# A graph-attention layer on one core: one shared tile for the gathered rows of eight quads, in place of a pool of eight buffers

## The chip, the core and the metric

The kernel runs on one core of one Trainium2 chip. The time is that of the device for one execution, in microseconds (us). The kernel before took 2875.91 us, the median of three runs.

Names of engines: PE is TensorE (PEld its weight loads), DVE is VectorE, ACT is ScalarE, POOL is GpSimd, SP is SyncE, which issues most of the loads and stores.

## The reference

12500 nodes with 128 features, 200000 edges sorted by their destination, 64 features for each edge, four heads of 32. The layer computes, for each destination, a softmax over its edges and a weighted sum of the source rows:

```python
h = jnp.maximum(_layernorm(x), 0.0)
hn = (h @ W_node.T).reshape(num_nodes, H, HD)
e = (edge_features @ W_edge.T).reshape(num_edges, H, HD)
att = jnp.sum(jnp.concatenate([hn[src], hn[tgt], e], -1) * a, -1)
att = jnp.where(att > 0, att, 0.2 * att)
m = jnp.maximum(segment_max(att, tgt), 0.0)
ex = jnp.exp(att - m[tgt])
denom = segment_sum(ex, tgt) + (num_edges - deg)[:, None] * jnp.exp(-m)
out = x + segment_sum((ex / denom[tgt])[:, :, None] * hn[src], tgt)
```

## The kernel before

**Groups and quads.** The edges are cut into G = 392 groups of 511 edges and a place in front (GE = 512). A group's edges lie as J = 4 columns of 128 partitions. Four groups (QG) make a quad; there are nq = 98 quads. Destinations being sorted, a group's edges reach into a window of at most 96 nodes (WIN).

**Prologue.** The gathers of the first four quads (RAW) fetch rows of x itself, 64 of them. Meanwhile the node phase normalises all nodes, multiplies them by the weights and writes a table in HBM, with a row of ROW = 137 numbers for each node. From quad 4 on, gathers fetch rows of that table.

**Gathers.** `gather(q, rows, width)` issues one indirect DMA on POOL for each column of each group, 16 in a quad (L135). Each fetches 128 rows, as `srci` tells, into a tile `ga` of the pool `gath` (L129), which has eight buffers. The tile of quad q + 8 takes the place of quad q's. A tile that takes another's place waits until all that use the earlier one are done, so the first gather of quad q + 8 waits for the last use of quad q's tile; the other 15 follow in POOL's order. Nearly all that POOL does in the main loop is to issue these gathers.

**Logits.** `all_logits(q)` opens with `open_logits(q)`, which issues the loads of quad q + 2 on SP: `ea` and `db` (L281, L283), the four windows `pw` and `xw` (L466, L468), and its gathers on POOL. Each of its four steps then makes one group's marks `at` (L498, DVE) and its logits `lg` (L503, L506, PE). `add_sources(q)` adds the part that comes from the gathered rows (L518, L520, DVE). That is the first reader of a quad's gathers in the main loop.

**Softmax.** After each super, in the main part four quads, `softmax(s)` turns the logits, runs scans on DVE, and puts out the factors `ex_ps`, `xs` and `facs` that the sums use.

**Sums.** `sums(q)` takes the quad's groups in turn. For each one DVE multiplies the gathered rows by `ex` in place (L685) and writes the one-hot matrix `hot` (L689); PE multiplies the columns 1 to 3 into `acc` (L694). Column 0 carries over what the group before left unfinished, so `complete_group` follows one group later: DVE scales the carried row into `ga` (L633), ACT copies its count (L637), PE adds column 0 (L638), and ACT copies the sum out to `pt` (L639), from which the next group's carry is read. L638 is the last instruction that reads a group's part of `ga`. The chain L639, L633, L638, L639 goes from group to group. `divide` finishes a quad (L706 to L718), and SP stores four windows to `out` (L720).

**Order.** All engines run their instructions in the order in which the code issues them (`manual_schedule`); `together` deals out the steps of several generators in turn. In the main loop, a step of `sums` stands beside a step of `all_logits` of a quad four or five further on, and in the first quad of each super beside a step of the softmax too. Waits between engines are put in by the framework, from what each instruction reads and writes.

Of the kernel before, what the change touches and what calls it, by code (L numbers as in the profile page):

```python
# [8 lines left out]
F32 = mybir.dt.float32  # L9
# [6 lines left out]
P = 128  # L16
# [8 lines left out]
R_CNT, R_SRC, ROW = H * HW, H * HW + 1, H * HW + 5  # L25

J = 4
# [3 lines left out]
QG = 4  # L31
# [2 lines left out]
SIDE = PIECES * H  # L34
NODE_T = 9
RAW = 4
SETS = max(NODE_T, QG * J)
PAD = 1 << 20

# [6 lines left out]
def kernel(  # L46
# [41 lines left out]
    consts = ctx.enter_context(tc.tile_pool(name="consts", bufs=1))  # L88
# [30 lines left out]
    nq = len(quads)  # L119
    raw = RAW  # L120
    assert raw == 4 <= nq
    g_raw = sum(quads[raw - 1])
    gath = ctx.enter_context(tc.tile_pool(name="gath", bufs=8))
    GA = {}

    def gather(q, rows, width):

        g0, m = quads[q]
        ga = GA[q] = gath.tile([P, QG, J, ROW], F32, name="ga")  # L129
        for i in range(m):  # L130
            n = -(-min(E - (g0 + i) * NE + 1, GE) // P)
            if n < J:
                nc.vector.memset(ga[:, i, n:, :], 0.0)
            for j in range(n):
                nc.gpsimd.indirect_dma_start(  # L135
                    out=ga[:, i, j, 0:width], out_offset=None, in_=rows,
                    in_offset=bass.IndirectOffsetOnAxis(ap=srci[:, g0 + i, j:j + 1], axis=0))
# [8 lines left out]
    with tc.manual_schedule():  # L146

        nc.sync.dma_start(srci[:, :g_raw], src_by_edge[:, :g_raw])
        for q in range(raw):
            gather(q, x, D)  # L150
# [6 lines left out]
        with tc.tile_pool(name="prep", bufs=1) as prep, tc.tile_pool(  # L157
            name="prep_ps", bufs=1, space=bass.MemoryType.PSUM
# [21 lines left out]
        def statistics(pool, rows, T):  # L180


            assert nc.vector.BN_STATS_DIM == 6
            stats = pool.tile([P, SETS, 6], F32, name="stats")
            for t in range(T):
# [3 lines left out]
            two = stats[:, :T, :].rearrange("p t (o k) -> p t o k", k=3)  # L189
            both = pool.tile([P, SETS, 2], F32, name="both")  # L190
            nc.vector.tensor_tensor(both[:, :T, :], two[:, :, 0, 1:3], two[:, :, 1, 1:3], op=OP.add)
            apart = pool.tile([P, SETS], F32, name="apart")
            nc.vector.tensor_tensor(apart[:, :T], two[:, :, 0, 1], two[:, :, 1, 1], op=OP.subtract)
            nc.vector.scalar_tensor_tensor(apart[:, :T], apart[:, :T], D / 4, apart[:, :T],
                                           op0=OP.mult, op1=OP.mult)
            nc.vector.tensor_tensor(apart[:, :T], apart[:, :T], both[:, :T, 1], op=OP.add)
            rstd = pool.tile([P, SETS], F32, name="rstd")
            nc.scalar.activation(rstd[:, :T], apart[:, :T], AF.Sqrt, bias=eps, scale=1 / D)
            nc.vector.reciprocal(rstd[:, :T], rstd[:, :T])
            shift = pool.tile([P, SETS], F32, name="shift")  # L200
            nc.vector.scalar_tensor_tensor(shift[:, :T], both[:, :T, 0], -0.5, rstd[:, :T],
# [84 lines left out]
        with tc.tile_pool(name="node", bufs=2) as node, tc.tile_pool(  # L286
            name="node_ps", bufs=2, space=bass.MemoryType.PSUM
        ) as node_ps, tc.tile_pool(name="index", bufs=1) as index, tc.tile_pool(
            name="index_ps", bufs=1, space=bass.MemoryType.PSUM
# [146 lines left out]
    with tc.tile_pool(name="work", bufs=2) as work, \  # L436
# [33 lines left out]
        def fetch(q):  # L470
            if q not in EA:
                fetch_edges(q)
            fetch_windows(q)
            if q not in GA:
                gather(q, table, ROW)
# [537 lines left out]
```

## Time and profile before

| | |
|---|---|
| median of 3 runs | 2875.91 us (2864.28 to 2878.76) |
| the profiled execution's own time | 2883.22 us |
| its span, first to last instruction | 2881.3 us |
| busy: POOL, PE, DVE, ACT | 52%, 48%, 47%, 15% |
| granted clock of TensorE, mean | 0.539 |
| DMA, mean over the span | 104 GB/s |
| gathers from the table | 1502, mean 951 ns each on POOL |

In a row of the groups, the numbers after the bar are the busy time in us and the mean of one in ns; after the second bar stands the time that the engine was idle just ahead of such instructions, and what ended most of it. In a row of the waits, the three numbers are the total in us, the number of waits and the longest. In a timeline row, the first number is the start in us from the start of the span, the second the time in us; the idle time ahead of it and what ended that stand in brackets. A time on POOL for a gather is that of issuing it, not of the transfer.

### The profile page before, as it was taken

Reading aid. Unit: us, or ns where it says so; the run is one execution under the profiler, and the core shown is the slowest. Engines: PE = TensorE matmul, PEld = TensorE weight load, DVE = VectorE, ACT = ScalarE, POOL = GpSimd, SP = SyncE. Lnnn points to the kernel's source line nnn. Section 1 sums busy time; section 2 is a strip of 40 time slices with the busy share of each in tenths; the row PEclk is TensorE's granted clock in tenths of the full one; section 3 lists DMA queues with packets and bytes.
Section 4 is the critical chain, followed back from the end, with each engine's and each line's share of the span. In section 5 each row is a group of like instructions: output and inputs, shape, how many; then the busy total and the mean of one; then the engine's idle time right before and its main releaser. Section 6 shows DMA issues by size and latency. Waiting matters only on the chain.

```text
span 2881.3 us, 29151 instructions
## 1 busy us (share of the span) xinstructions
PE 1388.3 (48%) x7275; PEld 1250.2 (43%) x7275; DVE 1361.9 (47%) x3314; ACT 428.3 (15%) x1777; POOL 1509.0 (52%) x1608
## 2 busy tenths in 40 slices
PE   2524645445444454454454454444444544544466
PEld 1423544444444444344444444444444444443465
DVE  2524454444444454453454454454453544554477
ACT  1524111111111111111111111111110110111112
POOL 7152345555555455555555555556555556565612
PEclk9966555555555555555555555555555555555555
DMA  4333344444344343434444434434434434434330
GB/s 141 115 112 85 88 125 105 103 112 111 97 111 108 95 123 98 111 101 105 113 102 108 110 100 108 111 100 108 111 101 107 110 101 107 107 90 105 94 93 19
DMA packets 214493, 299.10 MB, mean 104 GB/s; under 512 B 86121, under 2 KB 162153, under 8 KB 204914
## 3 DMA queue, kind: packets, MB, share of 16 engines
q1 hardware_dynamic: 162512, 184.97, 23.6%
q0 software_dynamic: 50112, 109.65, 15.7%
q10 hardware_dynamic: 1698, 2.58, 0.3%
q8 instruction: 61, 1.00, 0.1%
q14 instruction: 110, 0.90, 0.1%
HBM read 270.49 MB, written 26.52 MB: 103 GB/s over the span
## 4 chain that ended last, share of the span: by engine, by line
another core or an unknown queue 25%; PE 13%; DVE 10%; issue 6%; ACT 2%; DMA 0%; ACTq 0%; DVEq 0%; SPq 0%; POOL 0%; POOLq 0%
PE acc L694 7%; PE lg L506 2%; PE acc L638 2%; DVE at L498 2%; DVE res L714 1%; DVE res L718 1%; ACT pt L639 1%; DVE ga L633 1%; DVE run L576 1%; DVE hot L689 1%; DVE ga L685 1%; PE lg L503 1%; DVE run L554 0%; PE acc L609 0%
## 5 line engine op out<-in xcount | busy, mean ns | idle before, releaser
L135 POOL DMA_INDIRECT ga<-table,srci x1502 | 1428.0, 951 | 1252.6 <-PE acc L638 711.2
L694 PE MATMUL acc<-ga,hot 128*97 128x137 f32 x2352 | 650.0, 448 | 737.6 <-ACT ga L678 592.5
L694 PEld LDWEIGHTS acc<-ga,hot 128*97 128x97 f32 x2352 | 519.3, 279 | 762.5 <-ACT ga L678 602.1
L633 DVE TENSOR_TENSOR ga<-pt,facs 1x132 f32<-1x132 f32 x384 | 111.2, 289 | 1010.9 <-ACT pt L639 799.0
L639 ACT COPY pt<-acc 97x137 f32<-97x137 f32 x392 | 107.1, 273 | 2058.5 <-remote 1328.2
L506 PE MATMUL lg<-wblk,ea 128*128 128x8 f32 x1568 | 405.9, 357 | 0.0
L506 PEld LDWEIGHTS lg<-wblk,ea 128*128 128x128 f32 x1568 | 378.4, 306 | 0.0
L638 PE MATMUL acc<-ga,hot 128*97 128x137 f32 x784 | 261.9, 437 | 168.4 <-issue 82.4
L503 PEld LDWEIGHTS <-at 96*128 96x128 bf16 x1568 | 214.4, 165 | 227.2 <-DVE at L498 136.0
L638 PEld LDWEIGHTS acc<-ga,hot 128*97 128x97 f32 x784 | 195.9, 282 | 182.8 <-issue 89.6
L685 DVE TENSOR_TENSOR ga<-ga,ex_ps 128x528 f32<-128x528 f32 x392 | 270.4, 690 | 8.6 <-PE ex_ps L599 8.2
L498 DVE TENSOR_TENSOR at<-const_ps,db 96x512 bf16<-96x512 f32 x392 | 267.1, 683 | 7.4 <-DMA db<-in_dst_dram 1.5
L503 PE MATMUL lg<-pw,at 96*128 96x12 bf16 x1568 | 169.3, 181 | 158.4 <-DVE at L498 113.6
L689 DVE TENSOR_TENSOR hot<-const_ps,slot 128x384 f32<-128x384 f32 x384 | 209.6, 546 | 0.0
L599 PE MATMUL ex_ps<-ident,ex 64*128 64x64 f32 (+2 forms) x112 | 18.6, 315 | 214.4 <-ACT ex L588 214.4
L599 PEld LDWEIGHTS ex_ps<-ident,ex 64*128 64x128 f32 (+2 forms) x112 | 13.8, 207 | 217.4 <-ACT ex L588 217.4
L373 PE MATMUL row_ps<-wcat,hT 128*128 128x137 f32 x198 | 41.9, 365 | 77.7 <-DVE hT L365 31.6
L637 ACT COPY ga<-pt 1x1 f32<-1x1 f32 x384 | 72.3, 188 | 10.4
L373 PEld LDWEIGHTS row_ps<-wcat,hT 128*128 128x128 f32 x198 | 35.5, 255 | 84.0 <-issue 44.6
L135 POOL DMA_INDIRECT ga<-in_x_dram,srci x64 | 60.6, 947 | 20.8 <-issue 19.2
L714 DVE TENSOR_TENSOR res<-pt,const_ps 96x512 f32<-96x512 f32 (+1 forms) x101 | 67.4, 667 | 7.3 <-DMA out_dram<-res 3.5
L718 DVE TENSOR_TENSOR res<-res,xw 96x512 f32<-96x512 f32 (+1 forms) x99 | 66.7, 674 | 3.4
(133 smaller groups left out, 1036.2 us busy)
## 6 DMA issues: line engine op xcount, KB each, us to landing
db<-in_dst_dram SPq DMA_DIRECT2D x98, 768.0 KB
ea<-in_edge_t_dram SPq DMA_DIRECT2D x98, 512.0 KB
ga<-table,srci POOLq DMA_INDIRECT x1502
xw<-in_x_dram SPq DMA_DIRECT2D x392, 48.0 KB
out_dram<-res SPq DMA_DIRECT2D x392, 48.0 KB
pw<-side SPq DMA_DIRECT2D x392, 2.2 KB
table<-row SPq DMA_DIRECT2D x9, 616.5 KB
xt<-in_x_dram SPq DMA_DIRECT2D x9, 576.0 KB
```

Of the source, the lines that this page charges most:

```text
L135: nc.gpsimd.indirect_dma_start(out=ga[:, i, j, 0:width], out_offset=None, in_=rows, in_offset=bass.IndirectOffsetOnAxis(ap=srci[:, g0 + i, ...
L498: nc.vector.tensor_tensor(at[:, i, :], node_ps[0:WIN, g0 + i:g0 + i + 1].to_broadcast([WIN, GE]), db[:, i, :], op=OP.is_equal)
L503: nc.tensor.matmul(lg[:, i, j].rearrange("p k h -> p (k h)"), at[:, i, j * P:(j + 1) * P], sw, start=i + j == 0, stop=False, skip_group_ch ...
L506: nc.tensor.matmul(lg[:, i, 2 * w:2 * w + 2, 0, :], ea[:, i, w, :], wblk, start=False, stop=True, skip_group_check=True)
L633: nc.vector.tensor_tensor(ga[0:1, i, 0, 0:H * HW].rearrange("p (h w) -> p h w", w=HW), before[WIN:WIN + 1, 0:H * HW].rearrange("p (h w) -> ...
L638: nc.tensor.matmul(acc, hot[:, i, 0, :], ga[:, i, 0, :], start=False, stop=True)
L639: nc.scalar.copy(pt[:, i, :], acc)
L685: nc.vector.tensor_tensor(val, val, heads(ex)[:, :, :, g - s0].unsqueeze(3).to_broadcast([P, J, H, HW]), op=OP.mult)
L689: nc.vector.tensor_tensor(hot[:, i, :, 0:WIN], lane_ps.unsqueeze(1).to_broadcast([P, J, WIN]), slot[:, g, :].unsqueeze(2).to_broadcast([P, ...
L694: nc.tensor.matmul(acc, hot[:, i, j, :], ga[:, i, j, :], start=j == 1, stop=False)
L714: nc.vector.tensor_tensor(res[:, :n, :].rearrange("p g (h d) -> p g h d", d=HD), val[:, :, :, 0:HD], share_ps[:, :n, :].unsqueeze(3).to_br ...
L718: add.tensor_tensor(res[:, :n, :], res[:, :n, :], xw, op=OP.add)
```

## The change

The pool `gath` with its eight buffers goes. In its place one tile `ga_all` holds eight parts of a quad's size, and quad q takes the part q modulo 8. The dimensions of a part, and the bytes in all, are those of the eight buffers. Since all quads' rows now lie in one tile, the framework tells from the parts that instructions read and write who has to wait: a group's first gather waits for the uses of that group's place, not for those of the quad.

```diff
+QUADS = 8
...
-    gath = ctx.enter_context(tc.tile_pool(name="gath", bufs=8))
+
+    ga_all = consts.tile([P, QUADS, QG, J, ROW], F32, name="ga")
     GA = {}
 
     def gather(q, rows, width):
 
         g0, m = quads[q]
-        ga = GA[q] = gath.tile([P, QG, J, ROW], F32, name="ga")
+        ga = GA[q] = ga_all[:, q % QUADS]
         for i in range(m):
```

## The prediction

> **What bounds the kernel now.** I read the page first, then the waits, then the timelines of GpSimd and ScalarE over one quad, then the rows of line L520. The page:
>
> ```profile
> span 2881.3 us, 29151 instructions
> PE 1388.3 (48%) x7275; PEld 1250.2 (43%) x7275; DVE 1361.9 (47%) x3314; ACT 428.3 (15%) x1777; POOL 1509.0 (52%) x1608
> ...
> L135 POOL DMA_INDIRECT ga<-table,srci x1502 | 1428.0, 951 | 1252.6 <-PE acc L638 711.2
> ...
> L639 ACT COPY pt<-acc 97x137 f32<-97x137 f32 x392 | 107.1, 273 | 2058.5 <-remote 1328.2
> ```
>
> No engine is busy for much over half of the span, so waits set the time. ScalarE stands idle for 2058.5 us ahead of the copy L639, and most of that ends with "remote", which no instruction of this core explains. The waits by total:
>
> ```profile
> ACT pt L639 <- remote: 1328.2, 113, 18.6
> DVE ga L633 <- ACT pt L639: 800.6, 155, 14.4
> POOL ga L135 <- PE acc L638: 711.2, 80, 56.6
> ```
>
> VectorE waits behind L639 (L633 reads its output), and TensorE behind both. POOL's own long wait is the one that the change edits. One quad shows how these hang together; POOL first, then ACT:
>
> ```profile
> 1771.81 0.94 POOL L135 DMA_INDIRECT ga<-table,srci  x1 [5.80 <-PE acc L638]
> 1773.06 0.94 POOL L135 DMA_INDIRECT ga<-table,srci  x1 [0.30 <-issue]
> ...
> 1790.68 0.94 POOL L135 DMA_INDIRECT ga<-table,srci  x1 [0.30 <-issue]
> 1797.53 0.94 POOL L135 DMA_INDIRECT ga<-table,srci  x1 [5.90 <-PE acc L638]
> ```
>
> ```profile
> 1771.57 0.27 ACT L639 COPY pt<-acc 97x137 f32<-97x137 f32 x1 [1.67 <-PE acc L638]
> ...
> 1774.49 0.28 ACT L639 COPY pt<-acc 97x137 f32<-97x137 f32 x1 [2.18 <-PE acc L694]
> ...
> 1778.50 0.27 ACT L639 COPY pt<-acc 97x137 f32<-97x137 f32 x1 [3.51 <-PE acc L694]
> ...
> 1794.44 0.27 ACT L639 COPY pt<-acc 97x137 f32<-97x137 f32 x1 [15.45 <-remote]
> ...
> 1797.29 0.27 ACT L639 COPY pt<-acc 97x137 f32<-97x137 f32 x1 [1.67 <-PE acc L638]
> ```
>
> A quad's 16 gathers start together, 1.25 us apart, right after the last group of the quad eight before is summed. Three groups get through beside them, 2.9 to 4.0 us apart. The next matmul L638 ended at 1781.38, but L639, which waits for nothing except that matmul, started at 1794.44: 13.06 us later, 2.5 us after the burst of gathers was over (1790.68 + 1.25). For each of the 392 groups I took the time from the end of L638 to the start of L639. Its median is 0.04 us and the sum 1151 us, 40% of the span. It depends on the age of the unbroken burst when L638 ends: at 2 to 3 us the median is 0.04 (57 groups), at 6 to 7 it is 0.42 (56), at 8 to 9 it is 6.3 (27), at 9 to 10 it is 13.04 (51), at 12 it is 10.6 (4), at 18 it is 4.4 (6). From 9 us on, age plus delay is nearly always 22 to 23 us, that is the burst's 20.0 us and 2.6 more. So in a burst older than about 7 us TensorE's signal mostly stays out until POOL pauses. I call that the freeze; its cause I do not know.
>
> This makes a locked cycle: 20.0 us of gathers, 2.6 until the frozen signal arrives, 3.1 until the quad's last group is summed (1794.44 to 1797.53), which starts the next burst: 25.7 us for each plain quad, as 1771.81 to 1797.53 shows. Where a softmax lies in the quad (one in four) it is 32.4. Gathered data itself is late for nobody that matters. Of L520, the first reader of a gather:
>
> ```profile
> L520 DVE TENSOR_TENSOR U<-st,ga x98: 266/268/302, 260.0 to 2833.1; 128x64 f32<-128x64 f32 x98
> its engine sat idle before it (us, times) until:
>   ACT ga L261: 20.9, 1
>   DVE st L518: 0.6, 3
> ```
>
> **The change, part by part.** *Instructions.* Order and count on PE, DVE, ACT and SP stay as they are, and so do their waits; no transfer is added, moved or resized. SP's queue of loads and stores is untouched, and POOL's order too. The 1.1 MB of gathers a quad stay the same. The allocation is the same size and costs nothing at run time.
>
> *POOL's waits.* Before, the first gather of each of the 90 quads 8 to 97 waits for the L638 of the fourth group of the quad eight before. After, the first gather of each group (360) waits for the L638 of the same group there; the fourth group's wait is the old one. So the first three groups may start about 9, 6 and 3 us earlier within the fast part, or earlier still by the length of a freeze. Behind a waiting gather only later gathers are queued on POOL (and the last two quads' L662 and L718), and none is let go later than before. The built program has 271 more waiting instructions on POOL. The row of L135 gives 17 ns as the median of one (POOLq EVENT_SEMAPHORE x93: 17/17/43); 271 x 17 ns = 4.6 us, and they lie in POOL's idle time or in its 0.30 us gaps. Bounds 0 and 5 us; I take 0, since POOL idles for 5.8 us a quad. If that idle time is gone they cost the 5.
>
> *What early gathers do by themselves.* Nothing: L520 lost 0.6 us to them in 98. The Trainium skill says, in DMA: Bandwidth & Descriptors, section Issuing engines are not separate DMA queues, that issuing takes time that is usually small beside the transfer. The trace differs here: a quad's issue takes 20.0 us of POOL, while the page gives q0, the gathers' queue, 15.7% of 16 engines, 4.6 us of each quad (2881.3 x 0.157 / 98). By the rule only the landing counts, and the change is worth 0: 2883 us. By the row the issue itself sets the cycle, and its new shape has to be worked out.
>
> *What the new shape of the bursts does.* Start where a frozen signal arrives (time 0). It releases L639 and now also four gathers, 5.0 us. The next groups follow as the ACT timeline has them, 2.9, 2.9 and 4.0 us apart (mean 3.2): at about 3 and 6 us, each letting go four more gathers. At age 6 a signal is delayed by 0 to 0.5 us, so these two pass. The third comes at 9 to 10 us and freezes. POOL has twelve gathers: it stops at 15.0, and the frozen signal arrives at 17.6. Three groups in 17.6 us are 5.87 each, 23.5 for a quad instead of 25.7: 2.2 saved. The gain is the 3.1 us in which POOL waited for the fourth group after the signal was back, spread over a cycle of three groups. What is late next is the same signal again: the freeze stays, with shorter bursts. A third signal that slips through early (age 8 to 9, delay 6.3) joins the next four gathers to the burst: 22.6 us for four groups, 5.65 each, nearly the same.
>
> Does a freeze come sooner after a shorter pause? The new pause is 2.6 us. Ten bursts before follow pauses of 2.7 to 3.0 us instead of 5.6, and signals at ages of 4.1 and 6.1 still passed in 0.0 to 0.1 us. So I take no.
>
> The softmax quads: POOL is let go by groups further apart than its 5 us, so it pauses between. If they keep their whole extra time, they save 2.2; with no freeze left but the one ahead, their own steps as the timeline has them (3.4 + 5.5 + 9.2 after the delivery, and about 9 for the third group with a rest of freeze) make 27, a saving of 5.4. No row decides; I take the middle, 3.8.
>
> *The sum.* Four quads save 3 x 2.2 + 3.8 = 10.4 us; 90 quads make 22.5 fours: 234 us. The two open bursts of 64 gathers at the start (3.1 and 161.6) and the last eight quads have no such wait and keep their time. The profiled execution took 2883.2 us (its span of 2881.3 and 1.9 around it), 7 over the median of the runs, 2875.9. So 2649 against 2883, or 2642 us as the median.
>
> The Trainium skill also has a price for TensorE's signals: TensorE: Matmul & The Clock Gate, section The cost: per-tile semaphore tail, says that increments queue at about 26.3 ns each. A group's ten counts would then delay L639 by about 0.26 us, 392 groups by 0.10 ms, no burst would matter, and breaking it up would gain nothing (2883). The row says 0.04 us outside a burst and 13 in an old one; I go by the row.
>
> **The rivals.**
> 1. *Every group freezes (slower).* If after a short pause the freeze sets in before the next group is through (2.85 us), each group has four gathers and a wait: 5.0 + 2.6 = 7.6 us, against 6.43 now (25.7 / 4). That is 30.4 a quad, 90 x 4.7 = 423 us more: 3300. It turns to a loss once about one group in three goes so, (6.43 - 5.87) / (7.6 - 5.87). For it: POOL is issuing in a greater share of the time, and no burst before follows a whole run of short pauses. Against: the ten bursts above.
> 2. *The freeze takes the second group too.* Two groups in 12.6 us: 25.2 a quad, 0.5 saved, softmax quads 2: 3.5 a four, 79 us, 2797. For it: a few signals at 6.7 us were late by 1.9.
> 3. *No freeze is left.* If it needs many ready gathers in a row and not elapsed time, POOL's rate bounds: 20.0 a plain quad, 24.1 a softmax quad; 3 x 5.7 + 8.3 = 25.4 a four, 572 us: 2304. Against: groups come every 3.2 us while four gathers take 5.0, so POOL would soon run unbroken.
> 4. *The early gathers are hidden anyway.* The freeze follows something else that only coincides with the bursts, such as SP's issues of pw and xw: no change, 2876. Against: age plus delay is constant to 1 us.
>
> **How the numbers follow.** My case has 0.55, rival 2 0.13, rival 3 0.10, rival 4 0.05, rival 1, whole or in part, 0.17. Faster by over 0.5%, about what a measurement of this kernel can tell from no change: 0.78; within it 0.05; slower 0.17. The likeliest case alone, with softmax savings of 2.2 to 5.4 and late signals, spans 2560 to 2720. The range takes in rivals 2 and 4, the slow end of rival 3 and the mild end of rival 1: 2430 to 2900.
>
> **What would show it.** Right: GpSimd's timeline in runs of about 12 gathers, with waits ahead of the first gather of a group; plain quads 23 to 24 us apart; the "remote" wait of L639 still there, most waits 7 to 9 us and no longer 13 to 15; DVE, PE and SP busy times as they were. Wrong: freezes of L639 at burst ages under 4 us (rival 1), POOL unbroken and L639's waits gone (rival 3), or delays as long as before although POOL paused (rival 4).

## The result, and the profile after

The changed kernel takes 2566.27 us (median of four runs, 2556.94 to 2567.05) against 2870.1 us (2863.71 to 2878.76) for the kernel before, measured together: a ratio of 0.8932, 95% interval 0.8896 to 0.8968. The forecast was 2642 us, with a range of 2430 to 2900. On another chip, told further below, the same two kernels take 2051.0 and 2046.7 us, and the change is worth 0.2%; on two more the kernel before takes about 2050 us too. The gain belongs to the chip as much as to the kernel.

The page of the kernel after (every line of the code stands two lower than before: L641 is the old L639, L640 the old L638, L137 the old L135):

```profile
span 2564.4 us, 29422 instructions
PE 1396.5 (54%) x7275; PEld 1246.7 (49%) x7275; DVE 1360.6 (53%) x3314; ACT 427.9 (17%) x1777; POOL 1514.3 (59%) x1608
...
L137 POOL DMA_INDIRECT ga<-table,srci x1502 | 1433.4, 954 | 925.2 <-issue 404.5
...
L641 ACT COPY pt<-acc 97x137 f32<-97x137 f32 x392 | 107.1, 273 | 1662.7 <-remote 904.7
```

The busy times are those of before, within 9 us on each engine; only idle time went. POOL's idle time ahead of gathers fell from 1252.6 to 925.2 us, ScalarE's ahead of the copy from 2058.5 to 1662.7. The waits, by total, the number of them and the longest:

```profile
ACT pt L641 <- remote: 904.7, 103, 11.8
DVE ga L635 <- ACT pt L641: 468.5, 141, 11.1
...
POOL ga L137 <- remote: 226.6, 102, 3.3
```

"Remote" is still the first wait, but its longest is 11.8 us and not 18.6. The last row has grown: POOL itself now waits for a late signal 102 times and not 10, 226.6 us and not 32.3, but never for more than 3.3 us. Its old wait for L638, 711.2 us and up to 56.6 at a time, is down to 136.5 us and 13.8. GpSimd's timeline over one burst, then ScalarE's over the same time:

```profile
1629.80 0.94 POOL L137 DMA_INDIRECT ga<-table,srci  x1 [1.33 <-PE acc L640]
...
1643.68 0.94 POOL L137 DMA_INDIRECT ga<-table,srci  x1 [0.30 <-issue]
1647.17 0.94 POOL L137 DMA_INDIRECT ga<-table,srci  x1 [2.54 <-remote]
```

```profile
1629.57 0.27 ACT L641 COPY pt<-acc 97x137 f32<-97x137 f32 x1 [1.58 <-PE acc L640]
...
1632.48 0.27 ACT L641 COPY pt<-acc 97x137 f32<-97x137 f32 x1 [2.18 <-PE acc L696]
...
1636.49 0.27 ACT L641 COPY pt<-acc 97x137 f32<-97x137 f32 x1 [3.51 <-PE acc L696]
...
1646.93 0.27 ACT L641 COPY pt<-acc 97x137 f32<-97x137 f32 x1 [9.95 <-remote]
```

The burst that starts at 1629.80 has twelve gathers and ends at 1644.6. Three groups come through at 1629.57, 1632.48 and 1636.49; the fourth stays out until 1646.93, 2.3 us after the burst. The next burst starts 17.37 us after the first one. That is the cycle of the prediction, 17.6 us for three groups.

From here on "late time" is the time from the end of L638 to the start of L639, or of their counterparts, summed over the 392 groups; 14 us is its floor, 0.04 for each. (The end of a matmul is modelled in the profile. The same model gives the floor in every trace without gathers or from another chip.) A "burst" is a run of gathers with less than 0.9 us between them. "A four" is the mean time of four quads, from quad 21 to quad 84. All three are worked out from the starts and ends in the traces. A "signal" is the count that a finished matmul raises and that others wait for.

| kernel | late time | bursts, most frequent | a four |
|---|---|---|---|
| before | 1152 us | 89 of 16 | 108.7 us |
| after | 816 us | 69 of 12, 58 of 8, 20 of 4 | 94.7 us |

14.0 us saved in each of 22.5 fours is 315 us; the two profiled executions differ by 317 (2883.2 and 2566.2).

### The profile page after: what moved, and what is told of

Its sections match the earlier page's. It is cut to its first block, busy times and chain, and to the rows that moved or that the text cites. A ratio compares the mean times of both kernels' runs of the same rounds, so it can differ in the third digit from the quotient of the medians.

```text
span 2564.4 us, 29422 instructions
## 1 busy us (share of the span) xinstructions
PE 1396.5 (54%) x7275; PEld 1246.7 (49%) x7275; DVE 1360.6 (53%) x3314; ACT 427.9 (17%) x1777; POOL 1514.3 (59%) x1608
## 4 chain that ended last, share of the span: by engine, by line
another core or an unknown queue 31%; PE 19%; issue 17%; DVE 15%; ACT 5%; POOL 4%; SPq 2%; DMA 1%; DVEq 0%; ACTq 0%; POOLq 0%
PE acc L696 10%; POOL ga L137 4%; PE lg L508 4%; PE acc L640 3%; DVE at L500 2%; ACT pt L641 2%; DVE res L716 1%; DVE res L720 1%; DVE hot L691 1%; DVE ga L687 1%; DVE run L556 1%; DVE ga L635 1%; PE lg L505 1%; ACT ga L639 1%
## 5 line engine op out<-in xcount | busy, mean ns | idle before, releaser
L137 POOL DMA_INDIRECT ga<-table,srci x1502 | 1433.4, 954 | 925.2 <-issue 404.5
L696 PEld LDWEIGHTS acc<-ga,hot 128*97 128x97 f32 x2352 | 515.7, 278 | 372.1 <-ACT ga L680 168.5
L640 PE MATMUL acc<-ga,hot 128*97 128x137 f32 x784 | 265.6, 442 | 263.1 <-ACT ga L639 127.8
L641 ACT COPY pt<-acc 97x137 f32<-97x137 f32 x392 | 107.1, 273 | 1662.7 <-remote 904.7
L640 PEld LDWEIGHTS acc<-ga,hot 128*97 128x97 f32 x784 | 190.7, 279 | 291.8 <-ACT ga L639 142.1
L520 DVE TENSOR_REDUCE st<-lg 128x64 f32<-128x192 f32 x98 | 33.7, 344 | 124.7 <-remote 79.9
L601 PE MATMUL ex_ps<-ident,ex 64*128 64x64 f32 (+2 forms) x112 | 18.6, 315 | 110.5 <-ACT ex L590 65.4
L639 ACT COPY ga<-pt 1x1 f32<-1x1 f32 x384 | 72.4, 188 | 10.7
L137 POOL DMA_INDIRECT ga<-in_x_dram,srci x64 | 60.6, 947 | 20.8 <-issue 19.2
L601 PEld LDWEIGHTS ex_ps<-ident,ex 64*128 64x128 f32 (+2 forms) x112 | 13.8, 208 | 113.5 <-ACT ex L590 67.4
```

The lines of the kernel that those rows point to most:

```text
L137: nc.gpsimd.indirect_dma_start(out=ga[:, i, j, 0:width], out_offset=None, in_=rows, in_offset=bass.IndirectOffsetOnAxis(ap=srci[:, g0 + i, ...
L639: nc.scalar.copy(ga[0:1, i, 0, R_CNT:R_CNT + 1], before[WIN:WIN + 1, R_CNT:R_CNT + 1])
L640: nc.tensor.matmul(acc, hot[:, i, 0, :], ga[:, i, 0, :], start=False, stop=True)
L641: nc.scalar.copy(pt[:, i, :], acc)
L696: nc.tensor.matmul(acc, hot[:, i, j, :], ga[:, i, j, :], start=j == 1, stop=False)
```

## The experiments

The twelve kernels ran in four sets, each beside the kernel before on the same chip. The results number the chips. The first set ran on chip 7, where the kernel before took 2874.8 us. The runs of the result carry no number; their 2870.1 us for the kernel before are like chip 7's, and they are counted with it here. The others fell to chips 15, 8 and 6, where it took 2049.3, 2051.0 and 2051.4.

### Chip 7: is it the shape of the bursts?

**The same tile, with the old waits** (e1_last_first). The last group's gathers are put first, so that all 16 wait for the whole quad again.

```diff
-        for i in range(m):
+        for i in ((m - 1, *range(m - 1)) if q >= QUADS else range(m)):
```

> The changed kernel, but POOL issues a quad's gathers with the fourth group first. Its wait is the quad's last one, so all sixteen follow it together, as before the change; tile, count and bytes stay those of the changed kernel. If the shape of the bursts makes the gain (my theory): back to 2840 to 2890 us, bursts of 16, L641's long waits 13 us again. If the shared tile itself, or anything but the waits, makes it: 2550 to 2590 us.

Measured: 2866.53 us, 0.9978 of before (0.9956 to 1.0). Its row of the gathers and its first waits:

```profile
L137 POOL DMA_INDIRECT ga<-table,srci x1502 | 1432.0, 953 | 1232.1 <-PE acc L640 684.3
```

```profile
ACT pt L641 <- remote: 1248.7, 114, 18.0
POOL ga L137 <- PE acc L640: 684.3, 78, 60.7
```

89 bursts of 16 and a late time of 1120 us are back, and so are POOL's 684.3 us of waits for L640, the longest 60.7, and ScalarE's longest of 18.0. The tile is still shared, the instructions of PE, DVE, ACT and POOL are as many as in the changed kernel and differ only in order, and the gain is gone. It comes from the finer waits, not from the tile.

**Half of the change** (e1b_pairs). Groups are gathered in the order 1, 0, 3, 2, so that two go at a time.

```diff
-        for i in range(m):
+        for i in ((1, 0, 3, 2) if q >= QUADS and m == 4 else range(m)):
```

> The changed kernel, with the groups' gathers issued in the order second, first, fourth, third, so that eight are let go at a time. My cycle: the second group's signal comes back by 6 us, joins another eight to the burst, the third group freezes until about 22 us, and the fourth has to be summed before POOL may go on: about 25 us for four groups, 2780 to 2870 us, nearly all of the gain gone. If instead the time follows the mean wait that POOL is spared, half of the gain: about 2720 us.

Measured: 2708.12 us, 0.9424 (0.9381 to 0.9468); 69 bursts of 16, 41 of 8, late time 983 us, a four of 101.4. Half of the change brings half of the gain: the number of the second expectation, and more than my cycle allows. Quad by quad, each taken from one fourth L640's end to the next (medians), that expectation's reason does not fit. The two plain quads ahead of a softmax quad take 25.8 us each, unchanged, as the cycle says for pairs. The softmax quad and the next one take 22.5 and 26.9 where the same kernel with the old waits (e1_last_first) has 32.4 and 22.2, and the kernel before 32.4 and 25.7. Most of what this kernel gains, it gains where a softmax stretches the steps.

**No gathers** (e3_plain_loads). From quad 4 on, the 16 gathers of a quad are four plain loads of table rows on SP. The output is then not the layer's: the choice of rows is left out.

```diff
             for j in range(n):
+                if q >= RAW:
+                    if j == 0:
+                        t0 = (4 * (g0 + i)) % 96
+                        nc.sync.dma_start(ga[:, i, 0:n, :], by_tile(table, t0, n))
+                    continue
```

> The kernel before, but from quad 4 on the rows of a group come by one plain load on SP from consecutive rows of the table, in place of four gathers on POOL. The same bytes go over the same DMA engines, with four more issues on SP for each quad; the rows are the wrong ones, which leaves out the gathering. If POOL's run of gathers makes the freeze (my theory): the waits of L639 that end in remote fall from 1328 us to under 100, quads come 13 to 20 us apart, 1700 to 2100 us in all. If SP's issues or the DMA traffic make it: the delays stay, 2600 us and up.

Measured: 2014.73 us, 0.7016 (0.699 to 0.7042). Its waits:

```profile
...
ACT pt L644 <- PE acc L643: 1295.4, 392, 13.5
PEld L508 <- DVE at L503: 426.0, 98, 9.6
...
DVE res L719 <- DMA out_dram<-res: 313.1, 63, 8.3
```

No wait of L644 ends with "remote" any more; all 392 end with the matmul L643. The late time is 14 us, its floor. The next waits are TensorE's for VectorE's marks (L503) and VectorE's for the stores of `out` (L719). On this chip the late signals need the gathers.

**A short pause for each group** (e4_pause). One memset on POOL after each group's four gathers.

```diff
+    rest = consts.tile([P, 128], F32, name="rest")
...
+            if q >= QUADS:
+                for _ in range(1):
+                    nc.gpsimd.memset(rest, 0.0)
```

> The changed kernel, with one small memset on POOL after each group's four gathers[...], which breaks the run of gathers every 5 us. If a short break is enough to hold off the freeze: L641's remote waits under 200 us, a group each 5.5 us, 2400 to 2450 us. If the freeze goes by the share of time that POOL issues, or needs about 2 us of rest to clear: bursts lengthen by the memsets, 6.0 to 6.2 us a group, 2590 to 2650 us.

Measured: 2581.85 us, 0.8982 (0.8947 to 0.9017), late time 912 us, 87 bursts of 12. The memset takes 0.22 us and moved the gather behind it by only 0.08, because it lies in the gap of 0.30 us that follows every gather. It was no pause, the time lies between the two forecasts, and it decides nothing. A longer one was tried next, but the chip was another.

### Chip 15: no late signals at all

**Column 0 last** (e7_cols). A group's columns 1 to 3, free a little earlier than column 0, are gathered first.

```diff
-            for j in range(n):
+            for j in (*range(1, n), 0):
```

> The changed kernel with the columns of a group gathered in the order 1, 2, 3, 0. Columns 1 to 3 are read last by L696, which runs a group step before L640, so three of the four gathers are let go about 1 us sooner. My cycle counts gathers in a burst and the time after it, and neither changes: 2540 to 2590 us. If a finer release goes on paying: 2500 us or less.

Measured: 2045.7 us, 0.9978 (0.9967 to 0.9989) of a kernel before that takes 2049.3 us here. The late time is 14 us, and the 1502 gathers of the main part form one burst. The edit's own question can't be answered where no signal is late.

**Fewer bytes** (e8_narrow). Each gather from quad 8 on moves 16 numbers a row and not 137; the other columns keep earlier rows.

```diff
             for j in range(n):
+                at = slice(0, width)
+                if q >= 2 * RAW:
+                    at, rows = slice(ROW - 16, ROW), x.rearrange("n (k c) -> (n k) c", c=16)
                 nc.gpsimd.indirect_dma_start(
-                    out=ga[:, i, j, 0:width], out_offset=None, in_=rows,
+                    out=ga[:, i, j, at], out_offset=None, in_=rows,
```

> The changed kernel, but from quad 8 on each gather fetches 16 numbers of a row (64 bytes) and not 137 (548 bytes), taken from x; the other columns keep what was there. POOL issues as many gathers of as many rows. If the issue of the gathers makes the freeze: delays and cycles as in the changed kernel, 2500 to 2590 us. If the bytes that they move make it: the delays shrink with the bytes, 2300 us or less.

Measured: 2041.88 us, 0.9955 (0.9939 to 0.9972). POOL is busy for 1519.8 us, against 1521.4 in e7_cols with all the bytes: a gather's 1.25 us does not depend on its bytes.

**A long pause** (e5_pause10). Ten memsets in place of e4_pause's one.

> The changed kernel with ten memsets on POOL after each group's four gathers. The first of them lies in the gap of 0.30 us that follows a gather anyway (one memset in e4 took 0.22 us and moved the next gather by 0.08), so the rest is about 2 us. If the freeze needs an unbroken run of gathers and a rest of about 2 us clears it (my theory): L641 waits for L640 nearly never over 1 us, but a group takes at least 7.1 us, 90 x 4 x 7.1 = 2560 us for the gathered part, 2950 to 3050 us in all. If the freeze goes by the share of time that POOL issues (70% here): the delays stay near those of the changed kernel, 816 us in all.

Measured: 3036.25 us, 1.4805 (1.4775 to 1.4835). The bursts are four long, as meant, but there was no late signal for a pause to cure, and the pauses cost 2.8 us each (3.07 between two bursts in place of 0.30) on a POOL that has no idle time here.

**Seven parts** (e6_seven). `QUADS = 7`.

> The changed kernel with seven parts in the tile, not eight: a group's gathers wait for the group seven quads back, so they come a quad later as seen from their first reader. If only the shape of the bursts counts: 2555 to 2580 us. If the head start of the gathers over their readers had a part in the gain: over 2600 us, with waits on DMA ahead of L522.

Measured: 2644.8 us, 1.2911 (1.288 to 1.2941). With seven parts, the gathers of a quad stand in the code ahead of the sums that still need its place, so these sums take the rows of a quad seven later and wait for them. It is not the kernel with less room that I meant, and its time says nothing. Its trace does say something: it has 76 bursts of 16 with pauses of 6.1 us (median) between them, the shape of the kernel before on chip 7. In these bursts 121 matmuls L640 ended at an age of 12 us or more, and none of their signals was over 0.04 us late. So it is not the shape of the bursts that sets chip 15 apart.

### Chips 8 and 6: is chip 15 the odd one?

**The changed kernel again** (f1_after), unaltered, with f2_narrow (e8_narrow again) and f3_pause10 (e5_pause10 again).

> The changed kernel, unaltered, beside the kernel before on whatever chip is given. If the chip is like the first one (the kernel before near 2870 us): 2566 us, ratio 0.893, late signals of TensorE summing to about 816 us, bursts of 12, 8 and 4. If it is like the second one (the kernel before near 2049 us): no late signal (each under 0.1 us), POOL gathering without a pause, 20 us a quad, and 2044 to 2049 us, ratio 0.997 to 1.0; the gain of the change is then gone although every instruction is the same. If the gain came from the coarser release by itself and not from the late signals, the ratio is near 0.9 on any chip.

Measured: 2046.73 us, 0.9984 (0.9974 to 0.9994) of 2051.02. Of its page and its waits:

```profile
span 2044.7 us, 29422 instructions
PE 1366.3 (67%) x7275; PEld 1237.5 (61%) x7275; DVE 1363.9 (67%) x3314; ACT 428.0 (21%) x1777; POOL 1523.3 (75%) x1608
...
POOL 7577777777777777777777777777777777777774
...
L137 POOL DMA_INDIRECT ga<-table,srci x1502 | 1441.0, 959 | 469.4 <-issue 389.1
...
L641 ACT COPY pt<-acc 97x137 f32<-97x137 f32 x392 | 107.4, 274 | 1268.0 <-PE acc L640 1268.0
```

```profile
ACT pt L641 <- PE acc L640: 1268.0, 392, 14.0
...
DVE U L522 <- DMA ga<-table,srci: 424.8, 77, 12.2
```

The instructions are those of the 2566 us kernel, 29422 of them. The same row L641 has no "remote" at all. POOL's digits are 7 from end to end: 1441.0 us of gathers and 469.4 of gaps are 1910 of the 2044.7 us, 1.27 us for each of the 1502 gathers, which all lie in one burst. No signal is more than 0.04 us late in it. The data itself is now what VectorE waits for: 424.8 us ahead of L522, where the kernel before had no wait for a gather ahead of its counterpart L520 on the first chip. POOL has become the bound.

> The changed kernel with each gather of quad 8 and later moving 16 numbers a row in place of 137 (the other columns keep the rows of earlier quads), so a gather moves 8 KB and not 70 KB. On a chip with late signals: if the lateness comes from POOL's making of the gathers (1.25 us each, which e8_narrow showed does not depend on the bytes), bursts and delays stay and it takes 2540 to 2590 us; if it comes from the bytes on the way (the DMA rings or the memory filled), the delays go and it takes about 2045 us, the POOL bound. On a chip without late signals: 2042 us again, which tells nothing apart.

Measured: 2043.97 us, 0.9974 (0.9963 to 0.9986). As announced for a chip without late signals, it tells nothing more.

> The changed kernel with ten more memsets on POOL after every group's four gathers, which cost 2.6 us a group where no signal is late (3036 us). On a chip with late signals: if a signal comes out as soon as POOL is out of gathers for a moment (over 0.3 us), every burst is 4 gathers long, no signal is late by more than about 1 us, and the time is again 3036 us within 1%, though the same signals are late by 816 us in all without the pauses; if the gathers' number or bytes outstanding is what counts, and not their unbroken run, signals stay late by several us each and the time is 3150 us or more.

Measured: 3037.74 us, 1.4825 (1.48 to 1.485). It equals 3036 us within 1%, but with no late signal to remove this is no support for either reading.

**The old waits and fewer bytes together** (f4_last_narrow): the edits of e1_last_first and e8_narrow.

> The changed kernel with the last group's gathers first (so that a whole quad's gathers wait for the whole quad, as in the kernel before) and with 16 of 137 numbers a row moved from quad 8 on (the other columns keep the rows of earlier quads). On a chip with late signals (the kernel before near 2870 us): if POOL's unbroken run of gathers makes the signals late, 89 bursts of 16 and late signals of about 1120 us in all stay, and it takes 2850 to 2870 us; if the bytes on the way do, the delays go and it takes about 2045 us. On a chip without late signals (the kernel before near 2050 us): 2040 to 2055 us; and since 16 gathers take 20.0 us there and a plain quad's sums come free before POOL has issued the 16 gathers ahead of them, POOL should show pauses of under 2 us a quad even where it waits for whole quads, which would say why the change is worth at most 0.5% there.

Measured: 2047.82 us, 0.9973 (0.9957 to 0.9989), on chip 6. The bytes stay undecided, since nothing is late here either. The other half was answered:

```profile
POOL ga L140 <- issue: 449.3, 1474, 0.3
```

Even where 16 gathers wait for a whole quad, POOL stands still only for the gap of 0.3 us between two gathers: 1390 of them form one burst. Releasing places group by group offers POOL something that it doesn't need. That is why the change is worth 0.2% on a chip where no signal is late.

## Why the prediction was right, and what it did not know

*The locked cycle held.* Bursts of twelve start 17.4 us apart (median of 69; 17.6 forecast). Of the 86 late signals in them, 61 come 2.1 to 2.6 us after the last gather (2.6 taken), and 22 still come while the gathers run. Three groups in 17.4 us are 23.2 a quad, 2.5 saved for 2.2. The late signal is still what most cycles end with, as the prediction said.

*Some second signals did freeze* (rival 2, in part). I had taken signals at age 6 to pass; after the change the median delay is 0.5 us at age 6 to 7 (47 groups), but 5.9 at age 5 to 6 (22) and 9.7 at 7 to 8 (35). Most of the 58 bursts of eight come from these: 40 late signals lie in them. They cost no more than the others: 11.7 us for two groups, 5.85 each, and not rival 2's 12.6, since the next burst starts 1.7 us after they end and not 2.6.

*The mis-sized term is the softmax quad.* Three plain quads save 3 x 2.5 = 7.5 us, and the four saves 14.0, so 6.5 is left for the softmax quad. I had taken 3.8 between bounds of 2.2 and 5.4. The late time in a four says the same: it falls from 52.0 to 37.5 us, 6.4 of that in the three plain quads and 8.1 in the softmax quad (12.7 to 4.6), while the rest of the four stays at 56.7 and 57.2. So the softmax's own steps were not hidden; what went there is most of the lateness. e1b_pairs points the same way: its plain quads stay at 25.8 us (medians), and its four still saves 7.3. The division depends on where a quad is cut: from one fourth copy L641 to the next, the softmax quad saves 4.7 and the plain ones 9.3. The sum does not: 10.4 forecast and 14.0 measured, by 22.5 fours, make 81 us of the 83 by which 2649 missed the profiled 2566.2.

*The terms at nothing were at nothing.* 271 more waiting instructions cost nothing that shows, and PE, DVE and ACT are as busy as before. Of 131 groups at an age under 4 us, two froze (3.6 and 5.7 us); rival 1 needed one in three to make a loss. The 0.6 us that I counted as L520's loss to the gathers is a wait for `st`: in the lines shown, nothing ahead of L520 waits for a gather. TensorE's counts, of which I took ten for each group, are 2249 in all, under six for each; their price was smaller still, and no nearer to the row.

*The price of issuing.* The rule that I weighed, that issuing is usually small beside the transfer (the Trainium skill, DMA: Bandwidth & Descriptors, section Issuing engines are not separate DMA queues), would have made the change worth 0. It does not hold here: on chip 7 the issue's shape set the cycle, on the others its 1.27 us a gather is the bound, and e8_narrow shows that bytes don't change it. On chip 8 the change was worth nearly that 0, but for the opposite reason.

*Rival 3 exists, elsewhere.* "No freeze is left" happened on chips 15, 8 and 6. I priced it at 2304 us; POOL's rate gives 2047. I had kept 24.1 us for a softmax quad, but over a four POOL only has its 64 gathers to issue, 79.9 us, and the softmax quad's longer time (27.7) is made up for by a plain one of 13.6. The forecast was right for a chip with late signals, such as its trace came from. On chip 8 its gain of 8% would have been wrong, and nothing in one trace told the two apart.

*What stays open.* That the finer waits make the gain on chip 7 is shown (e1_last_first), and that the late signals there go with the gathers (e3_plain_loads). I called the cause an unbroken burst older than about 7 us. On the other three chips, bursts of 16, 1390 and 1502 gathers hold back nothing, so such a burst is not enough; something of the chip or its state at the time must join it. Chip 7 without gathers takes 2015 us, less than the others with them (2047), and POOL's gathers take 0.94 to 0.97 us on all four, so neither slow engines nor slow gathers is the difference. Whether chip 7's lateness follows bytes or issues, and whether a true pause ends it, was not answered: the runs meant for that fell to chips without it.

Three things in the traces narrow it down. First, the freeze is not a full stop. After the matmul L638 of 1781.38, the kernel before has counts of TensorE recorded at 1783.88, 1790.19, 1794.42 and 1794.51, and L639 started at 1794.44. Single counts still come out during a burst, and when it is over the rest follow 0.04 to 0.1 us apart. Second, TensorE is not alone. SyncE's register moves stretch as well (shortest, median and longest in ns; the first row is of the kernel before, the second of f1_after):

```profile
L466 SPq MOVE pw<-side x392: 2/29/1392, 164.1 to 2800.3; - x196
L468 SPq MOVE pw<-side x392: 29/29/38, 97.2 to 1953.2; - x196
```

Of the 2357 register instructions on SyncE (`MOVE` and `FUSED_REGOPS`), 420 took over 0.3 us in the kernel before, every one during a burst or within 2.6 us of its end; in e3_plain_loads and in each trace of the other chips none did. Third, the trace itself has gaps there: it holds 1874 of TensorE's 2249 counts before, but 2228 of 2249 in f1_after and 1308 of 1318 in e3_plain_loads. So what the gathers hold up on chip 7 is wider than TensorE's signal. Whether the recording of the profile has a part in it was not tested.

## What to carry to other kernels

When an instruction starts long after the only thing that it waits for, with "remote" in the profile, measure that delay against what other queues are doing, and test by reshaping them: here the same gathers in bursts of mostly 12 and 8 instead of 16 gave 10.7%. Then repeat on another chip before the gain is called the kernel's: on chip 8 it was 0.2%. And where gathers are many and small, count them: 16 gathers at 1.25 us are 20.0 us of GpSimd for each quad, whatever their bytes. On the chips without late signals only fewer gathers, not earlier ones, could help, and not by much: e3_plain_loads, which has none from quad 4 on, still took 2015 us (on chip 7) against their 2047.

## What the runs showed of the hardware that was not expected

- One program, the kernel before, takes 2875 us on one chip and 2049 to 2051 on three others. The kernel after was traced on both sorts, and there the granted clock is the same (0.540, and 0.535 in f1_after) and the busy times agree within 2.3%. The 520 us between these two traces are idle time, with 816 us of late signals on the one and 14, the floor, on the other. (The gap is less than the 802 us between these, since POOL sets the pace on the other.)
- On the chip with late signals, taking the gathers away restores 0.04 us a signal; the delays reach 14.0 us with them in the kernel before. SyncE's register moves, 29 ns otherwise, take up to 1.39 us during the same bursts.
- An indirect gather of 128 rows takes about 0.95 us of GpSimd and a gap of 0.30, with 70 KB as with 8 KB. A memset of 0.22 us in that gap delays the next gather by 0.08.
